# Layer 0 of a four-layer convolution chain: key transposes for two parts together, perceptron outputs for two images together

## The chip, the cores and the metric

The kernel runs on one core of one Trainium2 chip. The metric is the device time of one launch in microseconds; the time before is the median of three runs, 6786.55 us (6781.14 to 6790.85). TensorE (PE in the profile) multiplies matrices and writes its products to PSUM, eight banks of 512 float32 columns on 128 partitions. ScalarE (ACT) and VectorE (DVE) read the banks, apply functions, and write to SBUF. SyncE (SP) issues the transfers.

## The reference

The input x is (4, 16, 512, 512) in float32, four images of 16 channels. Four layers follow one another. Layer 0, the one that the change touches, is attention in windows of 8 by 8 pixels with a perceptron behind it:

```python
pos = conv(x, pos_w, feature_group_count=16)            # 3x3 depthwise
x = x + pos + pos_b
y = _aff(xt, alpha1, beta1, color1)                     # tokens, 16 channels
qkv = win @ qkv_w.T + qkv_b                             # windows of 64 tokens, 2 heads of 8
attn = softmax(einsum('bhnd,bhmd->bhnm', q * hd**-0.5, k))
out = einsum('bhnm,bhmd->bhnd', attn, v) @ proj_w.T + proj_b
x = shortcut + out
h1 = gelu(_aff(x, alpha2, beta2, color2) @ fc1_w.T + fc1_b)   # 64 hidden
x = x + (h1 @ fc2_w.T + fc2_b)
```

Layers 1 to 3 are 3x3 convolutions with quantisation and batch normalisation, with a residual, and with a pixel-wise perceptron. They stand after layer 0 and are left as they are.

## The kernel before

`window_attention` computes layer 0 in 64 steps. A step covers all four images (index u) and, in each, four strips (index vv) of one row of windows, 64 columns wide; a tile of y has 128 partitions and, for each image, 512 columns (eight windows of 64 tokens).

**The order is written by hand.** `tc.manual_schedule` keeps the order of the program on PE, DVE, ACT and SP. Each engine takes its instructions in that order, and an instruction that waits holds what is behind it.

**PSUM.** Banks 0 to 3 are two pairs (`pairs`), banks 4 to 7 are single tiles. The pairs hold the scores, the queries and the depthwise sums. The single banks change their use during the step: `attend(k)` puts weighted values into bank 4 or 6 and sums into bank 5 or 7 (4 and 5 for even k), `values(k)` puts transposes into the same bank as the weighted values of k, `project` uses all four, `hidden` takes 4, 5 and 6 in turn, and `output` has bank 7.

**One step n in order of the program.**

1. The table for exp and ln is loaded on ScalarE (L475). `values(0)`: four transposes of the keys (`y2`, matmuls with 128 rows and 128 columns of the array) into a bank (L348), which VectorE copies to `yt` (L353). `scores(0)`: 16 matmuls of 32 rows by 128 columns into the four pair banks (L361; each float32 matmul that is no transpose shows as two records), then two exponentials on ScalarE (L369), one for each pair.
2. `output` for the last quarter of the step before (`last`): four matmuls of 128 rows by 32 columns into bank 7 (L429), added to y by VectorE (L431).
3. Seven turns, k = 1 to 7. Each: `scores(k)`, then `attend(k-1)` (L380 weighted values and L385 sums, both 128 rows by 32 columns), then `values(k)`, then `divide(k-1)`: Ln and Exp of the sums on ScalarE (L394, L395), the product on VectorE (L396). In turn 3 VectorE also takes a maximum over y (L489). In odd turns SP issues the turned keys of the next step (L320).
4. The queries of the next step (L330), the last `attend` and `divide`, and `project` (L404), whose results VectorE adds to y (L409).
5. The perceptron, 52 places long: at 16 of them `hidden` (four matmuls of 32 by 32 into one bank, L418, then a Gelu on ScalarE, L423), at 36 of them `depthwise` for step n + 2 (four matmuls of 32 by 32, L297). A hidden unit comes at every third place. After the sixth and the tenth hidden unit stands an `output`.
6. `position(n + 2)`: the depthwise sums leave the pair banks for y, images 1 and 3 by ScalarE (L308), 0 and 2 by VectorE (L312). Then `output` for the third quarter.

In odd steps each `output` is followed by `store`: VectorE takes a maximum of the finished image (L440) and SP issues eight stores (L447). In even steps SP issues the loads of x for a later pair of steps (L279).

A hidden unit lives in a tile with eight buffers; `xo`, the finished rows, has one, and y has three.

Of the kernel before, what the change touches and what calls it, by code (L numbers as in the profile page):

```python
# [11 lines left out]
F32 = mybir.dt.float32  # L12
BF16 = mybir.dt.bfloat16
AF = mybir.ActivationFunctionType
ALU = mybir.AluOpType
# [9 lines left out]
P = 128  # L25
# [6 lines left out]
WS = 8  # L32
# [106 lines left out]
def window_attention(ctx: ExitStack, tc, x, x1, hots, m, v, peak):  # L139
# [13 lines left out]
    nc = tc.nc  # L153
    U = V = 4
    BW = 64
    NJ = BW // WS
    N = NJ * T
# [11 lines left out]
    def bank(i):  # L169
        return pairs[i // 2][:, i % 2, :] if i < 4 else singles[i - 4]  # L170

    def quad(i):
        return slice(32 * i, 32 * i + 32)
# [74 lines left out]
    px = ctx.enter_context(tc.tile_pool(name="w0x", bufs=2))  # L248
# [37 lines left out]
    def by_window(ap):  # L286
        return ap.rearrange("p (j a x) -> p a j x", a=WS, x=WS)
# [4 lines left out]
    def depthwise(n, tap, u):  # L292

        dy, dx = divmod(tap, 3)
        at = BW * (n % 2) + dx
        for vv in range(V):
            nc.tensor.matmul(  # L297
                bank(u)[quad(vv)], taps[quad(u), tap, :],
                xts[n // 2][quad(u), vv, dy : dy + WS, at : at + BW],
                start=tap == 0, stop=tap == 8,  # L300
            )
# [15 lines left out]
    def turn_keys(y, vv):  # L317
        for u in range(U):
            for w in range(2):
                nc.sync.dma_start(  # L320
                    y2[32 * u + C * w : 32 * u + C * w + C, vv, :, w, :],
                    y[32 * vv + C * w : 32 * vv + C * w + C, u, :].rearrange(
                        "p (j t) -> p j t", t=T
                    ),
                )

    def queries(y, h):
        for u in range(U):
            for vv in range(V):
                nc.tensor.matmul(  # L330
                    bank(vv)[quad(u)], wg[h][quad(vv)], y[quad(vv), u, :],
                    start=True, stop=True,
                )
        for vv in range(V):
            out = g[:, vv, :, h, :]
            src = bank(vv).rearrange("p (j t) -> p j t", t=T)
            if vv % 2:
                nc.scalar.activation(out, src, AF.Identity, bias=gb[:, h : h + 1])
            else:
                nc.vector.tensor_scalar(out, src, gb[:, h : h + 1], None, ALU.add)  # L340


    def values(k, n):

        vv, jl = k // 2, 4 * (k % 2)
        b = bank(4 + 2 * (k % 2))
        for jj in range(4):
            nc.tensor.transpose(  # L348
                b[:, P * jj : P * jj + P],
                y2[:, vv, jl + jj].rearrange("p w t -> p (w t)"), m("ident"),  # L350
            )
        t = px.tile([P, 4, P], F32, tag="yt", name=f"yt{n}_{k}", bufs=3)
        nc.vector.tensor_copy(t.rearrange("p j c -> p (j c)"), b)  # L353
        return t

    def scores(k, n):

        vv, jl = k // 2, 4 * (k % 2)
        for jj in range(4):
            for u in range(U):  # L360
                nc.tensor.matmul(  # L361
                    bank(u)[:, P * jj : P * jj + P],
                    y2[quad(u), vv, jl + jj].rearrange("p w t -> p (w t)"),
                    g[quad(u), vv, jl + jj].rearrange("p h t -> p (h t)"),
                    start=True, stop=True,
                )
        e = px.tile([P, U, 4, P], F32, tag="e", name=f"e{n}_{k}", bufs=3)
        for i in range(2):
            nc.scalar.activation(  # L369
                e[:, 2 * i : 2 * i + 2].rearrange("p u j t -> p u (j t)"),  # L370
                pairs[i], AF.Exp,
            )
        return e

    def attend(e, yt, k):

        b, d = bank(4 + 2 * (k % 2)), bank(5 + 2 * (k % 2))
        for jj in range(4):
            for u in range(U):
                nc.tensor.matmul(  # L380
                    b[quad(u), P * jj : P * jj + P], yt[:, jj, quad(u)], e[:, u, jj, :],
                    start=True, stop=True,
                )
        for u in range(U):
            nc.tensor.matmul(  # L385
                d[quad(u)], own, e[:, u].rearrange("p j t -> p (j t)"),
                start=True, stop=True,
            )

    def divide(k, n):  # L390
        vv, jl = k // 2, 4 * (k % 2)
        b, d = bank(4 + 2 * (k % 2)), bank(5 + 2 * (k % 2))
        r = px.tile([P, 512], F32, tag="r", name=f"r{n}_{k}")
        nc.scalar.activation(r, d, AF.Ln)  # L394
        nc.scalar.activation(r, r, AF.Exp, scale=-1.0)  # L395
        nc.vector.tensor_tensor(  # L396
            o[:, vv, jl : jl + 4].rearrange("p j h t -> p (j h t)"), b, r, ALU.mult
        )
# [14 lines left out]
    def hidden(y, q, n):  # L413

        u, vv = q // 4, 3 * q % 4
        b = bank(4 + q % 3)
        for k in range(4):
            nc.tensor.matmul(  # L418
                b[quad(k)], fc1[quad(vv), quad(k)], y[quad(vv), u, :],
                start=True, stop=True,  # L420
            )
        hd = px.tile([P, N], F32, tag="hid", name=f"hid{n}_{u}_{vv}", bufs=8)
        nc.scalar.activation(hd, b, AF.Gelu, bias=f1b)  # L423
        return vv, hd

    def output(y, xo, hids, u, n):
        b = bank(7)
        for vv, hd in hids:
            nc.tensor.matmul(b[quad(vv)], m("fc2"), hd, start=True, stop=True)  # L429
        at = BW * (n % 2)  # L430
        nc.vector.tensor_tensor(  # L431
            xo[:, u, :, at : at + BW].rearrange("p a (j x) -> p a j x", x=WS),
            by_window(b), by_window(y[:, u]), ALU.add,
        )
        if n % 2:
            store(xo, n // 2, u)

    def store(xo, k, u):
        i, cb = divmod(k, NQ)
        nc.vector.tensor_reduce(  # L440
            peak[:, U * k + u : U * k + u + 1], xo[:, u], AX.XY, ALU.max,
            apply_absolute_value=True,
        )
        for vv in range(V):
            for w in range(2):
                r = SR * (2 * vv + w) + WS * i
                nc.sync.dma_start(  # L447
                    x1[u, r + 1 : r + 1 + WS, :, XW * cb : XW * cb + XW].rearrange(
                        "a c x -> c a x"
                    ),  # L450
                    xo[32 * vv + C * w : 32 * vv + C * w + C, u],
                )
# [19 lines left out]
    last, xo = None, None  # L472
    for n in range(STEPS + 1):
        if n < STEPS:
            nc.scalar.preload_act_table_set("natural_log_exp_and_others")  # L475
            yts = {0: values(0, n)}
            es = {0: scores(0, n)}
        if last:

            output(*last)  # L480
        if n == STEPS:
            break
        for k in range(1, 8):
            es[k] = scores(k, n)
            attend(es[k - 1], yts[k - 1], k - 1)
            yts[k] = values(k, n)
            divide(k - 1, n)
            if k == 3:
                nc.vector.tensor_reduce(  # L489
                    most[:, n : n + 1], ys[n], AX.XY, ALU.max, apply_absolute_value=True  # L490
                )
            if k % 2 and n + 1 < STEPS:
                turn_keys(ys[n + 1], k // 2)
        if n + 1 < STEPS:
            queries(ys[n + 1], 0)
        attend(es[7], yts[7], 7)
        divide(7, n)
        if n + 1 < STEPS:
            queries(ys[n + 1], 1)
        y = ys.pop(n)  # L500
        project(y)

        ahead = n + 2 < STEPS
        if ahead and n % 2 == 0 and n // 2 + 2 < STEPS // 2:
            xts[n // 2 + 2] = load(n // 2 + 2)
        if n % 2 == 0:
            xo = px.tile([P, U, WS, XW], F32, tag="xo", name=f"xo{n}", bufs=1)


        hids, taken = [], [0] * U  # L510
        for i in range(13 * 4):
            q, rest = divmod(i - 4, 3)
            if i >= 4 and rest == 0 and q < 16:
                hids.append(hidden(y, q, n))
                if q in (5, 9):
                    output(y, xo, hids[q - 5 : q - 1], q // 4 - 1, n)
            elif ahead:
                depthwise(n + 2, taken[i % 4], i % 4)
                taken[i % 4] += 1
        if ahead:  # L520
            ys[n + 2] = position(n + 2)
        output(y, xo, hids[8:12], 2, n)
        last = (y, xo, hids[12:], U - 1, n)

# [797 lines left out]
```

## Time and profile before

| what | value |
|---|---|
| time, median of three runs | 6786.55 us |
| span of the profiled execution | 6787.2 us |
| steps of layer 0 | 64, the last hidden unit at 3619 us |
| from the first transpose of a step to that of the next | 53.9 to 54.5 us in many steps, up to 58.5 us |
| transposes (L348), copies to yt (L353) | 512 blocks of four, 353.7 us of copies at 691 ns |
| exponentials (L369) | 1024 of 1021 ns |
| hidden matmuls (L418), Gelus (L423) | 8192 records, 1024 Gelus of 686 ns |
| additions of outputs (L431) | 256 of 691 ns |

A line of the timeline has the start, the length, the engine, the line of the program, the operation, what it writes and reads, how many instructions were merged, and in brackets the idle time before it with what ended it. Several matmuls run side by side on different parts of the array[...]; so the spacing of starts tells more than the sum of lengths. "issue" as a releaser means that the profile shows nothing that the engine waited for.

### The profile page before, as it was taken

The numbers are of one execution on the slowest core, as the hardware profiler recorded it, in microseconds if no ns is written. First come the engines' busy times: TensorE is split into PE (matmuls) and PEld (weight loads), VectorE is DVE, ScalarE is ACT, GpSimd is POOL, SyncE is SP. The second block draws the span as 40 slices with busy tenths as digits, with TensorE's granted clock in tenths as the row PEclk, the third lists the DMA queues.
The fourth block names the chain that finished last, engine by engine and source line by source line (L and its number), as shares of the span: only waits on it lengthen the run. The fifth ranks groups of instructions, "written<-read, shape, count | busy, mean of one in ns | idle before, by whom it ended". The sixth has DMA issues, their size and how long they took to land. (4 is left out here: it accounts for less than half of the span.)

```text
span 6787.2 us, 317928 instructions
## 1 busy us (share of the span) xinstructions
PE 6456.3 (95%) x146976; PEld 3304.6 (49%) x146976; DVE 3196.5 (47%) x4640; ACT 4215.1 (62%) x5738; POOL 10.3 (0%) x49
## 2 busy tenths in 40 slices
PE   7999999999999999999995569999999999999999
PEld 4555555555555555555552334444444444444443
DVE  2444444444444444444444764444444444444444
ACT  3777777777777777777774344555555555555553
POOL 0000000000000000000000000000000000000000
PEclk9999999999999999999996679999999999999999
DMA  6454555545454545455526962222222222322221
GB/s 72 63 66 65 63 69 63 70 61 69 63 66 62 66 63 66 64 63 68 62 43 131 212 137 72 77 77 78 83 79 78 79 79 79 82 79 78 78 62 46
DMA packets 759438, 514.79 MB, mean 76 GB/s; under 512 B 354128, under 2 KB 648656, under 8 KB 749904
## 3 DMA queue, kind: packets, MB, share of 16 engines
q1 hardware_dynamic: 757808, 493.95, 42.6%
q8 instruction: 1154, 18.91, 1.3%
q14 instruction: 188, 1.54, 0.1%
q10 hardware_dynamic: 288, 0.39, 0.0%
HBM read 225.28 MB, written 134.48 MB: 53 GB/s over the span
## 5 line engine op out<-in xcount | busy, mean ns | idle before, releaser
L1123 PE MATMUL tb<-y,mat 32*32 32x512 f32 x16384 | 1682.9, 597 | 10.4 <-ACT hid L1129 7.5
L1129 ACT ACTIVATE hid<-tb,vec 128x512 f32<-128x512 f32 x1280 | 877.9, 687 | 1229.8 <-PE tb L1123 1207.7
L369 ACT ACTIVATE e<-pair 128x1024 f32<-128x1024 f32 x1024 | 992.4, 1021 | 231.4 <-PE pair L361 230.8
L1131 DVE TENSOR_SCALAR hid<-tb,vec 128x512 f32<-128x512 f32 x768 | 576.6, 751 | 1168.1 <-PE tb L1123 852.8
L297 PE MATMUL pair<-x,taps 32*32 32x512 f32 x18432 | 1005.3, 605 | 35.0 <-issue 20.7
L418 PE MATMUL bank<-y,fc_e 32*32 32x512 f32 x8192 | 890.9, 609 | 10.4 <-issue 6.3
L423 ACT ACTIVATE hid<-bank,f1b 128x512 f32<-128x512 f32 x1024 | 679.6, 686 | 338.3 <-PE bank L418 319.1
L353 DVE COPY yt<-bank 128x512 f32<-128x512 f32 x512 | 353.7, 691 | 906.1 <-PE bank L348 905.8
L1123 PEld LDWEIGHTS tb<-y,mat 32*32 32x32 f32 x16384 | 503.7, 103 | 393.8 <-issue 231.8
L361 PE MATMUL pair<-g,y 32*128 32x128 f32 x16384 | 653.2, 285 | 40.7 <-ACT e L369 36.8
L914 PE MATMUL tb<-z,cw 32*32 32x512 f32 x12864 | 641.3, 602 | 3.5 <-ACT z L1060 2.7
L914 PE MATMUL tb<-q,cq 32*32 32x512 bf16 x12672 | 468.2, 483 | 185.0 <-issue 130.8
L914 PE MATMUL tb<-x,cw 32*32 32x512 f32 x12480 | 635.2, 598 | 1.7 <-ACT z L1060 1.5
L361 PEld LDWEIGHTS pair<-g,y 32*128 32x128 f32 x16384 | 540.3, 187 | 189.3 <-ACT e L369 107.5
L914 PE MATMUL tb<-h,cw 32*32 32x512 f32 x12672 | 628.2, 601 | 1.6 <-ACT z L1060 1.5
L297 PEld LDWEIGHTS pair<-x,taps 32*32 32x32 f32 x18432 | 447.7, 103 | 362.9 <-issue 244.1
L380 PE MATMUL bank<-e,yt 128*32 128x128 f32 x16384 | 555.5, 276 | 1.0 <-ACT r L395 0.9
L385 PE MATMUL bank<-e,hot 128*32 128x512 f32 x4096 | 534.4, 592 | 0.0
L1137 PE MATMUL tb<-hid,mat 128*32 128x512 f32 x4096 | 495.9, 602 | 0.9 <-DVE o L1143 0.9
L380 PEld LDWEIGHTS bank<-e,yt 128*32 128x32 f32 x16384 | 417.7, 109 | 108.5 <-DVE yt L353 52.8
L993 ACT ACTIVATE q<-tx,unround 128x512 bf16<-128x512 f32 (+1 forms) x333 | 313.8, 967 | 235.4 <-DVE tx L990 131.9
L431 DVE TENSOR_TENSOR xo<-bank,y 128x512 f32<-128x512 f32 x256 | 177.0, 691 | 563.8 <-PE bank L429 562.4
(154 smaller groups left out, 6542.0 us busy)
## 6 DMA issues: line engine op xcount, KB each, us to landing
tx<-x SPq DMA_DIRECT2D x520, 256.0 KB, 5.8
y<-y SPq DMA_DIRECT2D x2048, 32.0 KB, 2.1
x<-xo SPq DMA_DIRECT2D x1024, 64.0 KB, 2.1
xi<-x SPq DMA_DIRECT2D x1024, 64.0 KB, 2.6
out_dram<-o SPq DMA_DIRECT2D x64, 1024.0 KB, 4.3
x<-in_x_dram SPq DMA_DIRECT2D x496, 81.2 KB, 6.3
x<-in_x_dram SPq DMA_DIRECT2D x496, 80.6 KB, 6.4
tx<-x SPq DMA_DIRECT2D x8, 192.0 KB, 3.8
```

What stands on the lines that cost most here:

```text
L297: nc.tensor.matmul(bank(u)[quad(vv)], taps[quad(u), tap, :], xts[n // 2][quad(u), vv, dy : dy + WS, at : at + BW], start=tap == 0, stop=ta ...
L361: nc.tensor.matmul(bank(u)[:, P * jj : P * jj + P], y2[quad(u), vv, jl + jj].rearrange("p w t -> p (w t)"), g[quad(u), vv, jl + jj].rearra ...
L369: nc.scalar.activation(e[:, 2 * i : 2 * i + 2].rearrange("p u j t -> p u (j t)"), pairs[i], AF.Exp,)
L380: nc.tensor.matmul(b[quad(u), P * jj : P * jj + P], yt[:, jj, quad(u)], e[:, u, jj, :], start=True, stop=True,)
L385: nc.tensor.matmul(d[quad(u)], own, e[:, u].rearrange("p j t -> p (j t)"), start=True, stop=True,)
L418: nc.tensor.matmul(b[quad(k)], fc1[quad(vv), quad(k)], y[quad(vv), u, :], start=True, stop=True,)
L423: nc.scalar.activation(hd, b, AF.Gelu, bias=f1b)
L914: nc.tensor.matmul(p[i][_quad(j)], weights[_quad(i), side, dx, :], src[side][_quad(i), j, dx : dx + W], start=side == 0 and dx == 0, stop= ...
L1123: nc.tensor.matmul(p[_quad(c)], w1[_quad(b), 1 - par, 32 * c : 32 * c + 32], inner(ys(mm + par))[_quad(b), s, :], start=True, stop=True,)
L1129: nc.scalar.activation(hd, p, AF.Relu, bias=v("l3_b1"))
L1131: nc.vector.tensor_scalar(hd, p, v("l3_b1"), 0.0, ALU.add, ALU.max)
L1137: nc.tensor.matmul(out_bank[_quad(b), :], w2[:, par], hd, start=par == 0, stop=par == 1)
```

## The change

Two kinds of blocks stand alone among work that divides TensorE's array in another way: the transposes (128 by 128) between `attend` (128 by 32) and `scores` (32 by 128), and the outputs (128 by 32) within the hidden and depthwise stream (32 by 32). The change puts two of each together, so that the array changes its division less often.

- Keys: in odd turns `values` runs for k and k + 1, in even turns not at all. The banks follow: `values(0)` uses bank 4, odd k bank 6, even k bank 7.
- Outputs: one `output` now covers two images, on banks 7 and 6, four matmuls each, with both additions (and in odd steps both maxima and stores) behind. It stands after the eleventh hidden unit for images 0 and 1, and behind the first scores of the next step for images 2 and 3. The output at the step's end is gone from there.
- Hidden units therefore take two banks in turn, 4 and 5, and their tile has twelve buffers, as up to eleven are alive at once.

```diff
--- before.py
+++ after.py
@@ -343,7 +343,7 @@
     def values(k, n):
 
         vv, jl = k // 2, 4 * (k % 2)
-        b = bank(4 + 2 * (k % 2))
+        b = bank(4 if k == 0 else 7 - k % 2)
         for jj in range(4):
             nc.tensor.transpose(
                 b[:, P * jj : P * jj + P],
@@ -413,27 +413,32 @@
     def hidden(y, q, n):
 
         u, vv = q // 4, 3 * q % 4
-        b = bank(4 + q % 3)
+        b = bank(4 + q % 2)
         for k in range(4):
             nc.tensor.matmul(
                 b[quad(k)], fc1[quad(vv), quad(k)], y[quad(vv), u, :],
                 start=True, stop=True,
             )
-        hd = px.tile([P, N], F32, tag="hid", name=f"hid{n}_{u}_{vv}", bufs=8)
+        hd = px.tile([P, N], F32, tag="hid", name=f"hid{n}_{u}_{vv}", bufs=12)
         nc.scalar.activation(hd, b, AF.Gelu, bias=f1b)
         return vv, hd
 
-    def output(y, xo, hids, u, n):
-        b = bank(7)
-        for vv, hd in hids:
-            nc.tensor.matmul(b[quad(vv)], m("fc2"), hd, start=True, stop=True)
+    def output(y, xo, hids, half, n):
+
+        banks = (bank(7), bank(6))
+        for k, (vv, hd) in enumerate(hids):
+            nc.tensor.matmul(
+                banks[k // 4][quad(vv)], m("fc2"), hd, start=True, stop=True
+            )
         at = BW * (n % 2)
-        nc.vector.tensor_tensor(
-            xo[:, u, :, at : at + BW].rearrange("p a (j x) -> p a j x", x=WS),
-            by_window(b), by_window(y[:, u]), ALU.add,
-        )
-        if n % 2:
-            store(xo, n // 2, u)
+        for k, b in enumerate(banks):
+            u = 2 * half + k
+            nc.vector.tensor_tensor(
+                xo[:, u, :, at : at + BW].rearrange("p a (j x) -> p a j x", x=WS),
+                by_window(b), by_window(y[:, u]), ALU.add,
+            )
+            if n % 2:
+                store(xo, n // 2, u)
 
     def store(xo, k, u):
         i, cb = divmod(k, NQ)
@@ -483,7 +488,11 @@
         for k in range(1, 8):
             es[k] = scores(k, n)
             attend(es[k - 1], yts[k - 1], k - 1)
-            yts[k] = values(k, n)
+
+            if k % 2:
+                for kk in (k, k + 1):
+                    if kk < 8:
+                        yts[kk] = values(kk, n)
             divide(k - 1, n)
             if k == 3:
                 nc.vector.tensor_reduce(
@@ -512,15 +521,14 @@
             q, rest = divmod(i - 4, 3)
             if i >= 4 and rest == 0 and q < 16:
                 hids.append(hidden(y, q, n))
-                if q in (5, 9):
-                    output(y, xo, hids[q - 5 : q - 1], q // 4 - 1, n)
+                if q == 10:
+                    output(y, xo, hids[0:8], 0, n)
             elif ahead:
                 depthwise(n + 2, taken[i % 4], i % 4)
                 taken[i % 4] += 1
         if ahead:
             ys[n + 2] = position(n + 2)
-        output(y, xo, hids[8:12], 2, n)
-        last = (y, xo, hids[12:], U - 1, n)
+        last = (y, xo, hids[8:16], 1, n)
```

## The prediction

> **What bounds the kernel now.** I read the page's first part, then the timeline of TensorE and of ScalarE inside one step of the attention layer (the change touches nothing else), then the waits over the 64 steps.
>
> ```profile
> PE 6456.3 (95%) x146976; PEld 3304.6 (49%) x146976; DVE 3196.5 (47%) x4640; ACT 4215.1 (62%) x5738; POOL 10.3 (0%) x49
> ```
>
> TensorE is busy all the time, but its ends are modelled, so this does not say that it is full. The stages do. First the attention loop, TensorE and then ScalarE, over the same microseconds (start, length, line, count, wait before):
>
> ```profile
> 1968.60 0.66 PE L348 MATMUL bank<-mat,y 128*128 128x128 f32 x4
> 1969.18 1.17 PE L361 MATMUL pair<-g,y 32*128 32x128 f32 x32
> 1970.29 1.08 PE L380 MATMUL bank<-e,yt 128*32 128x128 f32 x32
> 1971.19 1.04 PE L385 MATMUL bank<-e,hot 128*32 128x512 f32 x8
> 1972.16 0.66 PE L348 MATMUL bank<-mat,y 128*128 128x128 f32 x4
> 1972.74 1.17 PE L361 MATMUL pair<-g,y 32*128 32x128 f32 x32
> ```
>
> ```profile
> 1970.39 1.94 ACT L369 ACTIVATE e<-pair 128x1024 f32<-128x1024 f32 x2 [0.40 <-PE pair L361]
> 1972.29 0.60 ACT L394 ACTIVATE r<-bank 128x512 f32<-128x512 f32 x1
> 1972.92 0.63 ACT L395 ACTIVATE r<-r 128x512 f32<-128x512 f32 x1
> 1973.95 1.94 ACT L369 ACTIVATE e<-pair 128x1024 f32<-128x1024 f32 x2 [0.40 <-PE pair L361]
> ```
>
> One turn takes 3.56 us (1969.18 to 1972.74): scores 1.11, values times weights 0.90, sums 0.97, transposes 0.58. TensorE never waits here, but look how near it is: the exponentials of these scores end at 1970.39 + 1.94 = 1972.33, and only then are the pair banks free for the next scores, which start at 1972.74. The transposes fill that time; the slack is 0.4 us.
>
> Then the perceptron, ScalarE's column of one odd step:
>
> ```profile
> 1945.96 1.27 ACT L423 ACTIVATE hid<-bank,f1b 128x512 f32<-128x512 f32 x2
> 1947.40 2.91 ACT L423 ACTIVATE hid<-bank,f1b 128x512 f32<-128x512 f32 x4 [0.18 <-PE bank L418]
> 1951.78 0.69 ACT L423 ACTIVATE hid<-bank,f1b 128x512 f32<-128x512 f32 x1 [1.46 <-PE bank L418]
> ...
> 1956.23 0.69 ACT L423 ACTIVATE hid<-bank,f1b 128x512 f32<-128x512 f32 x1 [1.11 <-PE bank L418]
> 1957.23 0.69 ACT L423 ACTIVATE hid<-bank,f1b 128x512 f32<-128x512 f32 x1 [0.32 <-PE bank L418]
> 1958.22 1.94 ACT L423 ACTIVATE hid<-bank,f1b 128x512 f32<-128x512 f32 x3 [0.30 <-PE bank L418]
> 1960.45 0.69 ACT L423 ACTIVATE hid<-bank,f1b 128x512 f32<-128x512 f32 x1 [0.29 <-PE bank L418]
> 1961.07 1.27 ACT L308 ACTIVATE y<-pair,vec 128x512 f32<-128x512 f32 x2
> 1962.35 1.28 ACT L475 ACT_TABLE_LOAD   x1
> 1963.65 1.94 ACT L369 ACTIVATE e<-pair 128x1024 f32<-128x1024 f32 x2
> ```
>
> From the first Gelu to the start of the sixteenth: 14.49 us. The gaps of 1.46 and 1.11 us are the two outputs inside the stream. From the last Gelu on ScalarE runs without a gap into the exponentials of the next step: its chain, not TensorE's, sets the step's end. TensorE at that place:
>
> ```profile
> 1960.46 1.06 PE L429 MATMUL bank<-hid,mat 128*32 128x512 f32 x8
> 1961.46 0.66 PE L348 MATMUL bank<-mat,y 128*128 128x128 f32 x4
> 1962.05 1.50 PE L361 MATMUL pair<-g,y 32*128 32x128 f32 x32
> 1963.48 1.07 PE L429 MATMUL bank<-hid,mat 128*32 128x512 f32 x8
> ```
>
> The scores at 1962.05 stretch to 1.50 us instead of 1.17: they wait for y's last bank (L308 ends at 1962.34).
>
> **What the Trainium skill says.** "TensorEngine Tiling (Array Packing)", Key Properties: changing the tiling mode drains TensorE. The trace agrees: an L429 block of 1.06 us lies alone among 32*32 work, and an L348 block of four transposes costs 0.58 us although its four matmuls start 0.17, 0.11 and 0.11 us apart. "PSUM — Partial Sum Buffer", PSUM bank collisions: access to a bank is to be guarded bank by bank, so a matmul into a bank waits for the reader of its last contents. The trace agrees: scores held for the exponentials (104 us in all in L361's waits on L369) start 0.05 us after the exponential's end. "ScalarE: Activation LUTs", What ACT_TABLE_LOAD costs: about 280 ns + 0.833 ns per column, 93 ns of overlap back to back, so an estimate of 0.71 us for 512 columns and a pitch of 0.61; the trace has 0.69 and 0.59, which I use.
>
> **The change part by part.**
>
> *Transposes in pairs.* In turns 2, 4 and 6 the transposes vanish and join those of turns 1, 3 and 5. Four more transposes in the same mode cost 4 x 0.11 = 0.44 us, so a pair of turns should drop from 7.12 to 7.12 - 0.58 + 0.44 = 6.98. But in the empty turn the sums hand over straight to the next scores: ready 1.11 + 0.90 + 0.97 = 2.98 us after the scores' start S, whereas the exponentials end at S + 1.21 + 1.94 = S + 3.15. The first matmuls, into the first pair of banks, may go; those into the second pair wait to S + 3.20 and need 1.09 us from there (as in the step's first turn, where 28 matmuls resume at 1965.64 and L380 follows at 1966.73). The next block starts at S + 4.29, not S + 4.09: 0.20 us given back. A pair becomes 6.98 + 0.20 = 7.18, so **+0.06 us, three times a step: +0.2 us**. VectorE's second copy (0.69 us) ends about 1 us before the sums that need its bank; Ln and Exp end just as the next exponentials are due. Both cost nothing, hidden by TensorE's blocks. Bounds: -0.46 us a step if nothing waits (three times 0.15), +0.7 if the late exponentials delay ScalarE as well.
>
> *Two banks for the hidden layer instead of three.* The added wait: L418 for unit q+2 writes the bank that Gelu q reads. Behind it in TensorE's queue stand the depthwise matmuls, and ScalarE waits for its product. A hidden unit takes 1.21 us from first matmul to Gelu start when nothing is in its way (L418 at 1950.57, Gelu at 1951.78), Gelu 0.69, release 0.05: 1.95 us per bank, two banks, 0.975 us per unit. Today the six Gelus before the first output are about 0.75 us apart. In the starts of this trace, hidden unit q+2 precedes the end of Gelu q by 0.4 to 0.66 us for ten of the fourteen q (the four free ones lie behind an output). So the wait binds nearly everywhere.
>
> Even units from the first Gelu = 0: Gelu 2, 4, ... 10 start at 1.95, 3.90, ... 9.75. (Before, the eleventh started at 1956.23 - 1945.96 = 10.27, with two outputs on the way.)
>
> *One output of two images in the stream.* Now the double output: it starts 0.97 us after the first matmul of the unit before it (1952.94 to 1953.91), the next unit 1.05 us after the output's start, and 0.90 more for four more matmuls (in L380 as many columns, 1024 per column tile, take 0.90): 2.92 us. Unit 10's matmul is at 9.75 - 1.21 = 8.54, so Gelu 11 starts at 8.54 + 2.92 + 1.21 = 12.67. Gelu 12 follows 1.02 later (as 1951.78 to 1952.80), Gelu 13 at 12.67 + 1.95 = 14.62, Gelu 14 at 15.64, Gelu 15 at **16.57, against 14.49: +2.1 us**. The saved output is in this sum (0.5 us better at unit 10, 0.9 worse at unit 11).
>
> *The output at the step's end moves behind the next scores.* There it takes 1.06 + 0.90 instead of 1.06 us: from 1963.48 to about 1965.4, still before the exponentials' end at 1965.59, for which the next scores wait anyway. Where it stood it hid behind ScalarE's chain (y, table load, exponentials), which does not get shorter: worth 0 in odd steps. In even steps, in which the last Gelu to the exponentials takes 3.1 us on average instead of 2.48, TensorE is sometimes late there; I credit 0.4 us. The doubled additions and maxima on VectorE (2 x 0.69 + 2 x 1.22 us) lie in stretches where it idles, 4 us in the stream; the eight store issues that move fit before the keys of the next step. Twelve hidden buffers instead of eight make no wait.
>
> *Even steps.* They span 15.6 us from first to last hidden unit against 14.6 in odd ones, with TensorE gaps of up to 3.1 us for "issue" (L297's waits). I let half of that 1.0 us hide behind the new bank wait: -0.5.
>
> Sum: odd 2.1 + 0.2 = 2.3; even 2.1 - 0.5 + 0.2 - 0.4 = 1.4; 32 x 3.7 = 118 us. **6786.6 + 118 = 6905 us.**
>
> **The rivals.**
>
> *Drains win.* If neither bank wait nor exponentials bind, a step saves 0.46 (keys), 0.5 (one drain in the stream) and the 1.0 us of the output at the end: 64 x 1.96 = 125 us, **6661**. For it: TensorE is 95% busy and drains are real. Against it: the starts above, and ScalarE's gapless chain at the end.
>
> *The bank wait binds only half.* If depthwise matmuls ahead of the held unit keep the array as full as now, 1.0 us of the 2.1 stays; with 0.2 for the keys and 0.2 saved in even steps, 64 x 1.1 = 70: **6857**. For it: a unit with its two depthwise turns is 24 passes on 16 tiles, 0.67 us at 0.45 us a pass, less than the 0.975 that the banks allow, so there is room to catch up after an output.
>
> *Gains and losses cancel.* Keys at -0.46, the end's output at -0.5, the bank wait at +1.0: **6789**.
>
> *Worse.* All waits in full in even steps too and the upper bound for the keys: 64 x (2.1 + 0.7) = 179, **6966**.
>
> **How the numbers follow.** My forecast 0.62, half bind 0.18, worse 0.05, cancel 0.05, drains win 0.10. The range 6825 to 6955 leaves out cancel, drains win and the far end of worse. Faster 0.11, same 0.04, slower 0.85.
>
> **What would show it.** Right: L418 waiting on ACT L423 rises from 10 us to over 50; the first to the sixteenth Gelu takes some 16.5 us in odd steps; turns alternate between about 4.2 and 3.0 us with L361 waiting on L369 three times more per step; the exponentials follow the last Gelu by 2.5 us as now. Wrong: Gelus still 0.75 us apart, or the exponentials at the step's start nearer to the last Gelu.

## The result and the profile after

The changed kernel takes **6873.2 us** (median of four runs, 6865.1 to 6878.2) against 6787.4 us before (four runs), a ratio of **1.0126, 95% interval 1.0109 to 1.0144**: 86 us slower. The forecast was 6905 us with a range of 6825 to 6955. In the two profiles layer 0 ends (its last VectorE maximum) at 3627 us before and 3704 us after, +77 us. The layers behind it, whose code is the same, took 3160 and 3172 us; over all the kernels below they took 3158 to 3182 us in an order that follows no edit, so I read only the 77 us as the change.

The first view is ScalarE's timeline of one odd step of the kernel after, as it was shown of before (start, length, engine, line, operation, count, idle before and its releaser; the edits move line numbers a little, so that the output's L429 is L430 here and the table load's L475 is L480):

```profile
1985.55 1.26 ACT L423 ACTIVATE hid<-bank,f1b 128x512 f32<-128x512 f32 x2
1987.42 1.26 ACT L423 ACTIVATE hid<-bank,f1b 128x512 f32<-128x512 f32 x2 [0.60 <-PE bank L418]
1989.28 1.26 ACT L423 ACTIVATE hid<-bank,f1b 128x512 f32<-128x512 f32 x2 [0.60 <-PE bank L418]
...
1994.89 0.69 ACT L423 ACTIVATE hid<-bank,f1b 128x512 f32<-128x512 f32 x1 [0.60 <-PE bank L418]
1997.87 0.69 ACT L423 ACTIVATE hid<-bank,f1b 128x512 f32<-128x512 f32 x1 [2.29 <-PE bank L418]
1998.93 0.69 ACT L423 ACTIVATE hid<-bank,f1b 128x512 f32<-128x512 f32 x1 [0.37 <-PE bank L418]
...
2001.85 0.69 ACT L423 ACTIVATE hid<-bank,f1b 128x512 f32<-128x512 f32 x1 [0.30 <-PE bank L418]
2002.44 1.25 ACT L308 ACTIVATE y<-pair,vec 128x512 f32<-128x512 f32 x2
2003.71 1.28 ACT L480 ACT_TABLE_LOAD   x1
2005.00 1.94 ACT L369 ACTIVATE e<-pair 128x1024 f32<-128x1024 f32 x2
```

The Gelus now come in twos every 1.87 us with 0.60 us of idle time after each two: the beat of two banks. The one gap of 2.29 us is the double output. First to sixteenth Gelu: 2001.85 - 1985.55 = 16.30 us, against 14.49. Behind the last Gelu the chain to the exponentials is as before (3.15 us from start to start, 3.20 in the step shown of before).

The even steps, in which the loads of x are issued, looked otherwise before. Two lines of ScalarE from such a step, before:

```profile
2010.76 0.69 ACT L423 ACTIVATE hid<-bank,f1b 128x512 f32<-128x512 f32 x1 [1.43 <-PE bank L418]
...
2015.13 1.46 ACT L423 ACTIVATE hid<-bank,f1b 128x512 f32<-128x512 f32 x2 [1.11 <-PE pair L297]
```

The 1.43 us are the second output. The 1.11 us have none behind them: in that stretch TensorE's weight loads (PEld) paused for 1.05 us, up to 2013.93, with "issue" as the releaser. This step needs 15.79 us from first to sixteenth Gelu. The same place in an even step after, where the gap is gone and the whole stream takes 16.31 us, like that of an odd step:

```profile
1943.82 0.69 ACT L423 ACTIVATE hid<-bank,f1b 128x512 f32<-128x512 f32 x1 [0.30 <-PE bank L418]
1944.76 0.69 ACT L423 ACTIVATE hid<-bank,f1b 128x512 f32<-128x512 f32 x1 [0.25 <-PE bank L418]
1945.75 0.69 ACT L423 ACTIVATE hid<-bank,f1b 128x512 f32<-128x512 f32 x1 [0.30 <-PE bank L418]
```

What TensorE's weight loads wait for, over the 64 steps (us in total, times, longest), first before, then after:

```profile
PEld pair L297 <- issue: 217.1, 464, 3.1
...
PEld pair L361 <- ACT e L369: 104.3, 124, 1.1
...
PEld bank L418 <- ACT hid L423: 10.2, 11, 2.5
```

```profile
PEld bank L418 <- ACT hid L423: 266.7, 536, 0.7
PEld pair L361 <- ACT e L369: 203.7, 243, 0.8
...
PEld pair L297 <- issue: 140.1, 486, 1.6
```

The two that rose are the new waits: for the Gelu that still reads a bank, and for the exponentials that still read the pairs. The third, the gaps for "issue", fell.

TensorE in the attention turns of the kernel after:

```profile
1951.99 1.08 PE L380 MATMUL bank<-e,yt 128*32 128x128 f32 x32
1952.89 1.04 PE L385 MATMUL bank<-e,hot 128*32 128x512 f32 x8
1953.86 1.09 PE L348 MATMUL bank<-mat,y 128*128 128x128 f32 x8
1954.88 1.17 PE L361 MATMUL pair<-g,y 32*128 32x128 f32 x32
1955.98 1.08 PE L380 MATMUL bank<-e,yt 128*32 128x128 f32 x32
1956.88 1.04 PE L385 MATMUL bank<-e,hot 128*32 128x512 f32 x8
1957.85 1.39 PE L361 MATMUL pair<-g,y 32*128 32x128 f32 x32
```

The eight transposes take 1.02 us (1953.86 to 1954.88) where two blocks of four took 1.16. In the empty turn the sums go straight over to the scores, but these stretch to 1.39 us instead of 1.17: they wait in mid-block. The next L380 starts at 1959.17, so the two turns take 3.99 + 3.19 = 7.18 us, against 7.12.

At the step's end:

```profile
2001.84 0.66 PE L348 MATMUL bank<-mat,y 128*128 128x128 f32 x4
2003.17 1.74 PE L361 MATMUL pair<-g,y 32*128 32x128 f32 x32 [0.67 <-ACT y L308]
2004.83 1.92 PE L430 MATMUL bank<-hid,mat 128*32 128x512 f32 x16
2006.69 1.47 PE L361 MATMUL pair<-g,y 32*128 32x128 f32 x32
```

The output that stood ahead of the transposes is gone, and in its place TensorE idles 0.67 us for y (L308), so nothing is gained there. The double output of 1.92 us fits behind the scores.

### The profile page after: what moved, and what is told of

Same layout as the page of the kernel before. It is cut to its first block, busy times and chain, and to the rows that moved or that the text cites. A ratio compares the mean times of both kernels' runs of the same rounds, so it can differ in the third digit from the quotient of the medians.

```text
span 6876.4 us, 317929 instructions
## 1 busy us (share of the span) xinstructions
PE 6549.5 (95%) x146976; PEld 3320.6 (48%) x146976; DVE 3160.7 (46%) x4640; ACT 4184.5 (61%) x5738; POOL 10.2 (0%) x49
## 5 line engine op out<-in xcount | busy, mean ns | idle before, releaser
L297 PE MATMUL pair<-x,taps 32*32 32x512 f32 x18432 | 1073.4, 605 | 18.9 <-DMA x<-in_x_dram 13.3
L418 PE MATMUL bank<-y,fc_e 32*32 32x512 f32 x8192 | 931.0, 607 | 3.6 <-ACT hid L423 2.2
L361 PE MATMUL pair<-g,y 32*128 32x128 f32 x16384 | 693.1, 286 | 46.6 <-ACT y L308 40.1
L361 PEld LDWEIGHTS pair<-g,y 32*128 32x128 f32 x16384 | 582.5, 186 | 320.9 <-ACT e L369 215.2
L396 DVE TENSOR_TENSOR o<-bank,r 128x512 f32<-128x512 f32 x512 | 352.1, 688 | 531.9 <-PE pair L361 399.9
L380 PE MATMUL bank<-e,yt 128*32 128x128 f32 x16384 | 555.7, 276 | 1.2 <-ACT r L395 0.9
L353 DVE COPY yt<-bank 128x512 f32<-128x512 f32 x512 | 335.3, 686 | 480.5 <-PE bank L348 480.5
L380 PEld LDWEIGHTS bank<-e,yt 128*32 128x32 f32 x16384 | 417.8, 110 | 108.6 <-DVE yt L353 52.8
```

The lines of the kernel that those rows point to most:

```text
L297: nc.tensor.matmul(bank(u)[quad(vv)], taps[quad(u), tap, :], xts[n // 2][quad(u), vv, dy : dy + WS, at : at + BW], start=tap == 0, stop=ta ...
L361: nc.tensor.matmul(bank(u)[:, P * jj : P * jj + P], y2[quad(u), vv, jl + jj].rearrange("p w t -> p (w t)"), g[quad(u), vv, jl + jj].rearra ...
L380: nc.tensor.matmul(b[quad(u), P * jj : P * jj + P], yt[:, jj, quad(u)], e[:, u, jj, :], start=True, stop=True,)
L418: nc.tensor.matmul(b[quad(k)], fc1[quad(vv), quad(k)], y[quad(vv), u, :], start=True, stop=True,)
```

## The experiments

My theory: the loss is the bank wait, plus a little from the pairs of transposes, which in the empty turn wait for the exponentials. The main rivals: the doubled outputs themselves make the loss; or what counts is how often the array changes its division, so that the pairs gain. Each time below is a median, with the recorded ratio to the kernel before on the same chip and its 95% interval (medians before: 6777 to 6784 us; the recorded ratio differs from that of the medians by less than 0.001). The granted clock was 0.969 to 0.975 in all the profiles, so it does not order the kernels. Averages of odd or even steps are of steps 4 to 59.

**e1, pairs of transposes alone.**

```diff
-        b = bank(4 + 2 * (k % 2))
+        b = bank(4 if k == 0 else 7 - k % 2)
...
-            yts[k] = values(k, n)
+            if k % 2:
+                for kk in (k, k + 1):
+                    if kk < 8:
+                        yts[kk] = values(kk, n)
```

> The kernel before with the transposes in pairs alone (odd turns for k and k+1, banks 4, 6, 7); hidden units on three banks and four outputs as before. Theory (exponentials bind in the empty turn): exp of turn 0 to exp of turn 7 24.6 us instead of 24.54, to the projection 0.1 us more, in all +0.18 us a step, 64 steps: +12 us, about 6799. Rival (array changes are what counts): 0.15 us saved for each of three pairs, -0.46 us a step, -29 us, about 6757.

6799.8 us, 1.0026 (1.0016 to 1.0036): slower, as the theory has it. The exponentials of turn 0 to 7 are 24.61 us apart (24.54 before), and to the projection 6.32 us (6.21): +0.18 us a step. Saving array changes did not save time here.

**e2, two banks alone.**

```diff
-        b = bank(4 + q % 3)
+        b = bank(4 + q % 2)
```

> The kernel before with the hidden units on banks 4 and 5 instead of 4, 5, 6, and nothing else; four outputs and transposes as before. Theory (bank wait): even Gelus 1.87 us apart, first to sixteenth Gelu about 16.2 us in odd steps against 14.5, and the gaps for issue in even steps partly hidden; +1.0 to +1.8 us a step, +65 to +115 us, 6850 to 6900. Rival (the doubled outputs make the loss, not the banks): less than +15 us, below 6802.

6871.1 us, 1.0128 (1.0113 to 1.0142). Two banks alone cost about as much as the whole change. First to sixteenth Gelu is 11.51 + 1.00 + 3.86 = 16.37 us in odd steps, in the beat of 1.87 us between outputs. The rival that the doubled outputs make the loss falls: none is in this kernel.

**e3, the change without the pairs of transposes.** `values` as in the kernel before, the rest as changed.

> The changed kernel with the transposes single again, as before; outputs in twos and hidden units on two banks as changed. Theory: 12 us less than the changed kernel (6873), about 6861. Rival (array changes count): 29 us more than the changed kernel, about 6902.

6864.1 us, 1.0124 (1.0109 to 1.0138); 9 us below the changed kernel by the medians, in the direction of the theory and near its 12. The interval alone would not tell 9 us; the turns do: 24.55 and 6.20 us again. Beside e2 the doubled outputs save only 7 us, inside the noise: as long as two banks set the pace they are worth next to nothing.

**e4, doubled outputs with three banks for hidden units.** As e3, and

```diff
-        b = bank(4 + q % 2)
+        b = bank(4 + (q if q < 11 else q + 1) % 3)
```

> As e3, but the hidden units keep three banks: 4, 5, 6 in turn up to the eleventh unit, whose following output takes banks 7 and 6 (bank 6 was last used by the ninth unit), then 4, 5, 6, 4, 5. Theory (bank wait is the loss): Gelus 0.75 us apart again, first to eleventh 7.5 us, the gap at the output 3.0, the rest 3.2 to 3.5: 13.7 to 14.0 us against 14.5 before; with the end of even steps some 0.5 us better -0.7 to -1.2 us a step, -45 to -75 us, 6712 to 6742. Rival (doubled outputs make the loss): still above 6840. Rival (TensorE's stream is full anyway): 6770 to 6790.

6731.6 us, 0.9922 (0.9909 to 0.9935): 50 us *faster* than before, 132 us from e3 by one line. First to sixteenth Gelu: 7.47 + 3.01 + 3.31 = 13.79 us in odd steps. The wait is nearly gone from TensorE's list (267.6 us in e3):

```profile
PEld bank L418 <- ACT hid L423: 15.7, 24, 1.3
```

So the doubled outputs gain, and the third bank need not be given up for them. Bank 6 is free in time when the double output wants it (1.92 us, as in the changed kernel), and again two units later.

**e5 and e8, e4's gain in two halves.** e5 moves only the output of the step's end (as the change does), e8 joins only the two outputs in the stream; both keep three banks. The cut shows e8's edit; e5 leaves the two outputs of the stream alone and gives `output_two` the hidden units 8 to 15 behind the next scores.

```diff
-                if q in (5, 9):
-                    output(y, xo, hids[q - 5 : q - 1], q // 4 - 1, n)
+                if q == 10:
+                    output_two(y, xo, hids[0:8], n)
```

> The kernel before with the output of the step's end moved alone: images 2 and 3 come together behind the next scores on banks 7 and 6, the two outputs in the stream stay single on bank 7, hidden units on three banks, twelve buffers. Theory (ScalarE's chain from the last Gelu to the exponentials sets the step's end): nothing in odd steps, 0.3 to 0.6 us in even ones, -10 to -20 us, 6762 to 6772. Rival (TensorE sets it): the 1.0 us of the block is saved in every step, -64 us, about 6717.

> The kernel before with the two outputs of the stream alone put together behind the eleventh hidden unit (banks 7 and 6), three banks for hidden units as in e4, outputs of the step's end single and in place as before. Theory: first to sixteenth Gelu 13.8 us instead of 14.5 in odd steps, as in e4; -0.5 to -0.7 us a step, -30 to -45 us, 6736 to 6751. Rival (e4 gained at the step's end): 6765 to 6790.

e5: 6759.6 us, 0.9966 (0.9955 to 0.9978). From the last Gelu to the exponentials odd steps still need 3.17 us, even ones 3.59 on average instead of 3.82. It is somewhat better than the 10 to 20 us forecast, as the stream of the even steps shortened too. e8: 6744.1 us, 0.9938 (0.9923 to 0.9953), 13.79 us in the stream of odd steps, as forecast. The two halves, -24 and -40 us, add up to more than e4's -50, because both shorten the same even steps: their stream took 15.78 us before, 15.08 in e5, 15.11 in e8 and 14.78 in e4, where the two savings by themselves would give 14.41. In e4 and e8 the end of the odd steps takes 3.40 us instead of 3.17, which takes back part of the gain.

**e6, the whole change with three banks** (e4's line in the changed kernel).

> The changed kernel with its hidden units on three banks, as e4 has them; transposes in pairs. Theory (the parts add): e4 plus the loss of the pairs, 6732 + 12 to 18 = 6744 to 6750. Rival (the pairs cost only where the stage before is late): 6732 or less.

6754.8 us, 0.9956 (0.9941 to 0.9971): 23 us above e4, where 12 to 18 were forecast: 5 more than e1's loss, which is inside the noise. The change as a whole is a gain of 29 us once the hidden units keep their bank.

**e7, outputs in the attention turns.** If the empty turns wait for the exponentials, something should stand there; and an output divides the array as the sums do (128*32), so that right behind the sums it needs no change. (Cut: the output behind the first scores, those in turns 2 and 4, and the removed one of the stream. The hidden units take banks 4, 5 and 6 in turn.)

```diff
+            output(*last[:3], (0, 1), (7, 6), last[3])
...
+            elif last and k < 6:
+                output(*last[:3], (1 + k // 2,), (5,), last[3])
...
-                if q == 10:
-                    output(y, xo, hids[0:8], 0, n)
```

> e6 with no output in the stream: images 0 and 1 behind the first scores of the next step, image 2 in its turn 2 and image 3 in its turn 4, right behind the sums (the same division of the array), on bank 5, where the turns without transposes wait 0.2 us for the exponentials; sixteen hidden buffers, two buffers of exponentials instead of three. Theory: the stream loses its gap of 2.2 us over the pitch, turns 2 and 4 grow by 0.9 - 0.2 = 0.7 us each, in all -0.8 us a step against e6, -50 us, about 6695. Rival (the wait in the empty turns is not free time): +0.9 us each or more, 6715 to 6745. Rival (a stream without gaps backs up in the three banks): no better than e6.

**6654.9 us, 0.9808 (0.9794 to 0.9822)**: faster than both kernels by 129 and 218 us. TensorE in such a turn:

```profile
1907.10 1.08 PE L380 MATMUL bank<-e,yt 128*32 128x128 f32 x32
1907.99 1.04 PE L385 MATMUL bank<-e,hot 128*32 128x512 f32 x8
1908.85 1.04 PE L429 MATMUL bank<-hid,mat 128*32 128x512 f32 x8
1909.82 1.18 PE L361 MATMUL pair<-g,y 32*128 32x128 f32 x32
1910.93 1.08 PE L380 MATMUL bank<-e,yt 128*32 128x128 f32 x32
```

The output starts 0.86 us after the sums, and the scores behind it do not stretch: 1.18 us, the wait has been filled. The turn takes 3.83 us instead of 3.19, so 0.64 us for an output (0.7 forecast). The stream loses more than forecast: 11.32 us in both kinds of steps, against 13.79 and 14.84 on average in e6. I had taken 2.2 us from every step. Odd steps lose 2.47 us and even ones 3.52, as their gaps for issue are gone as well; that makes the 100 us instead of 50. Most of the gain is thus the stream without outputs; the filled wait is worth 0.2 us in each of two turns.

**e9 and e11, e7 with single transposes.** Do the pairs lose only where the turn is empty?

```diff
-            if k % 2:
-                for kk in (k, k + 1):
-                    if kk < 8:
-                        yts[kk] = values(kk, n)
-            elif last and k < 6:
+            if last and k in (2, 4):
                 output(*last[:3], (1 + k // 2,), (5,), last[3])
+            yts[k] = values(k, n)
```

> e7 with the transposes single, one block in each turn, as in the kernel before; outputs behind the first scores and in turns 2 and 4 as in e7. Theory (the pairs lose only where a turn is left empty and waits for the exponentials): in e7 turns 2 and 4 are filled, so there the pairs save 0.15 us each, turns 5 and 6 lose 0.06: taking them away costs 0.25 us a step, +16 us, about 6671. Rival (pairs of transposes lose whatever stands in the turn): taking them away saves 0.2 us a step, -12 us, about 6643.

6746.8 us, 0.9943 (0.993 to 0.9957): both sides missed by over 70 us. The trace names the cause, on VectorE and then on TensorE:

```profile
1951.66 0.69 DVE L434 TENSOR_TENSOR xo<-bank,y 128x512 f32<-128x512 f32 x1 [2.44 <-PE bank L429]
1952.39 1.22 DVE L443 TENSOR_REDUCE peak<-xo 128x1 f32<-128x1024 f32 x1
1953.52 0.68 DVE L353 COPY yt<-bank 128x512 f32<-128x512 f32 x1
```

```profile
1954.26 1.08 PE L380 MATMUL bank<-e,yt 128*32 128x128 f32 x32 [0.98 <-DVE yt L353]
```

The copy of this turn's keys stands behind the store's maximum, and TensorE waits 0.98 us for it (58.7 us in all, 60 times). In e7 this copy was made a turn earlier, together with its partner. e11 takes the maxima out of the way: the store of a single output comes after the turn's product, the maximum over y in turn 5 instead of turn 3.

> e9 with VectorE's long maxima out of the way of its copies: the store's maximum (1.22 us) in turns 2 and 4 behind the turn's product instead of ahead of its copy, the maximum over y (2.28 us) in turn 5 instead of 3. Theory (e9 lost 16 us to the drains of single transposes and the rest, some 75 us, to copies that come late behind these maxima): about 6671, exponentials of turn 0 to 7 26.3 us in both kinds of steps. Rival (single transposes cost this much by themselves): still above 6720.

6673.4 us, 0.984 (0.9824 to 0.9855): 73 us better than e9, and 18.5 us above e7, where 16 were forecast for the lost pairs. In even steps turn 0 to 7 takes 26.26 us (26.3 forecast) against 25.90 in e7, while the way to the projection is 0.11 us longer in e7; in odd steps it takes 26.40 us at the median, a little over the forecast. So the pairs gain 0.25 us in an even step where two of the three empty turns are filled (e7), and lose 0.18 where none is (e1). That e11 also moves the maxima does not disturb this: in its even steps each single output lengthens its turn by 0.86 us, the time that it takes by itself. The sign of their effect hangs on the wait for the exponentials.

**e10, the loads of x in odd steps.** In the kernel before,

```diff
-        if ahead and n % 2 == 0 and n // 2 + 2 < STEPS // 2:
+        if ahead and n % 2 and n // 2 + 2 < STEPS // 2:
```

> The kernel before with the loads of x issued in odd steps instead of even ones, nothing else. Theory (the gaps for issue in even steps come with the loads' transfers): odd steps now have a stream of 15.3 to 15.8 us from first to sixteenth Gelu, even steps 14.5; the total within 15 us of before. Rival (they belong to the steps themselves, such as the place in the program): even steps stay at 15.8 on average and odd ones at 14.5.

The gaps move with the loads: first to sixteenth Gelu 14.53 us on average in even steps and 15.45 in odd ones (15.78 and 14.49 before). The time is 6808.9 us, 1.0041 (1.0025 to 1.0056), 26 us more and so outside the 15 that I had given. In even steps the stream's start now comes 0.5 us later, and the cause of that stays open. In the profiles layer 0 ends only 5 us later than before, so most of the 26 us is not explained.

## Why the prediction was right, and where it was off

*Direction and mechanism* stood: the bank wait is the loss (e2 alone, and e4 and e6 without it), and ScalarE's chain keeps the output's removal at the step's end from paying in odd steps (0.67 us of idle TensorE in its place; in e5, which has this removal, odd steps still need 3.17 us there). The signs named ahead came too: the wait on L418 rose from 10 to 267 us, the exponentials follow the end of the last Gelu by 2.46 us, and the scores (L361) start 2.97 and 4.21 us apart in turn. One was smaller: L361 waits for the exponentials 243 times instead of 124, two more a step and not three. The pairs do add three a step (e1: 307 times), but behind the doubled output the wait in the step's first turn falls away (e3: 61 times).

*Transposes in pairs*: +0.2 us a step forecast, +0.18 measured (0.07 + 0.11), from two turns of 7.18 us, as worked out. e1 gave +18 us in time.

*Two banks*: the term was mis-sized by 0.3 us. I took 1.95 us per bank from a unit right behind an output (1.21 us to the Gelu); in the beat a unit needs 1.13 us (its first matmul 0.74, its Gelu 1.87 after the first Gelu of the step), so the beat is 1.87 us and the stream 16.30 instead of 16.57. Odd steps: +1.8, not +2.1. The double output's gap was right: 2.98 us from Gelu to Gelu, 2.92 forecast.

*Even steps*: the largest error. I let half of 1.0 us of issue gaps (the time in which TensorE waits for nothing that the profile shows) hide behind the bank wait. On average there were 15.78 - 14.49 = 1.29 us of them, and after the change 16.41 - 16.30 = 0.11 us was left: the bank wait did not come on top of them but in their place. Why the gaps themselves shrink is not shown. The stream of even steps grew by 0.63 us, not 1.6. The credit at their end was a little small: 3.82 to 3.23 us, -0.59 for -0.4.

The sum: odd 1.81 + 0.18 = 1.99, even 0.63 + 0.18 - 0.59 = 0.22; 32 x 2.21 = 71 us, beside 77 us to the end of layer 0 in the profiles and 118 forecast. Both errors made the loss too large; the range held without their cancelling.

*Rivals.* "Drains win" was wrong for this kernel, yet right in part about the outputs once they cost no bank: joining the two in the stream saves 0.70 us in the odd steps of e4 and e8, where it had 0.5, but the one at the step's end is not worth its 1.0 us (e5 gains 24 us, not 64). "Half bind" (6857) came nearer to the measured time than my forecast, but for another reason: the wait binds everywhere, and it takes the place of gaps that were there in every second step.

## What to carry to other kernels

Count the banks of a product before taking one away. Add up the time from its first matmul to the consumer's start, the consumer's own time and the release, divide by the number of banks, and compare with the pace at which TensorE delivers. Here 1.87 us over two banks is 0.94 us a unit against 0.75, while three banks, 0.62, sufficed. Joining blocks of one kind saves the change of the array's division, but the time that an engine no longer spends between two uses of a buffer may have been hiding another engine's work; put a block there that fits, as e7 does (0.2 us a turn). A long instruction on a queue in order belongs behind the short ones that somebody waits for.

## What the runs showed of the hardware

Dividing the array anew for 128*128 transposes costs little here: 0.14 us was saved when two blocks of four became one of eight (1.16 to 1.02 us). What an output costs hangs on its place. From first to sixteenth Gelu, odd steps take 11.32 us without an output in the stream (e7), 14.49 with two single ones (before) and 13.79 with one double one (e4, e8): 3.2 and 2.5 us for two images. Behind the sums (128*32 too) an output starts 0.86 us after them, and two of them lengthen the turns by 1.3 us. How much of the difference is the array's division and how much the order of the units around the output, the runs do not separate. TensorE's gaps for "issue" in the stream come with the loads of x (e10), up to 3.1 us each; in e7, whose stream has no outputs, they were nearly absent (12.3 us in all), though the same loads are issued in the same steps. Why is not settled.
